# Ten of fourteen own products a layer as three products of 12-bit parts, in a three-layer graph network

## The chip, the core and the metric

The kernel runs on one core of one Trainium2 chip. The metric is the device time of the whole kernel in microseconds (us), the median of several runs. Its engines work side by side, each through its own list of instructions in a fixed order: TensorE (PE in the profile) multiplies matrices, VectorE (DVE) and ScalarE (ACT) work element by element, GpSimd (POOL) and SyncE (SP) here mostly issue transfers (DMA). They wait for each other by semaphores.

## The reference

A layer norm and a relu of x (2500 nodes of 256 numbers), three graph convolutions over the given 80000 edges, and a product of the four stages' results with Wf, added to x. Cut to what matters:

```python
def _edge_conv(x, src, dst, W, b):
    xi, xj = x[dst], x[src]
    m = jnp.concatenate([xi, xj - xi], axis=-1) @ W + b
    s = jax.ops.segment_sum(m, dst, num_segments=N)
    cnt = jax.ops.segment_sum(jnp.ones((dst.shape[0],), m.dtype), dst, num_segments=N)
    return s / jnp.maximum(cnt, 1.0)[:, None]
for W, b in ((W0, b0), (W1, b1), (W2, b2)):
    h = jax.nn.relu(_edge_conv(h, src, dst, W, b))
    xs.append(h)
return x + jnp.concatenate(xs, axis=-1) @ Wf + bf
```

With A the matrix that counts the edges from node to node, a layer is the relu of A times (h Wb) / cnt plus h (Wt - Wb): the second term, a node's product with its own features, is what this text calls an **own product**.

## The kernel before, in words

The nodes are cut into five groups of up to 504; the last ("alone") has 486. Layer 0 builds A from sorted edges with matmuls of one-hot matrices and multiplies at once. It stores A in device memory, the groups 0 to 3 as bf16, the last as f32. Layers 1 and 2 read it back. Every f32 value that multiplies A is held as two f32r parts, `zh` (high) and `zl` (the rest), so that a product with A is two f32r matmuls.

Each of the layers 1 and 2 has two phases.

*The node turns* (`for i in range(Q + LAG)`, 12 turns for 10 pairs of node tiles). A turn multiplies 256 nodes' features by the layer's weights (`Nodes.multiply`, from parts that `split` has made two turns before), takes the results (`parts`, `combine`, `sums`: into zh, zl and their combinations sh, sl) and multiplies the lone group two turns behind (`Alone.multiply`). The lone group's blocks of A are loaded by `load_first` and `load_alone`.

*The stream* (`Stream.run`, 70 steps). The groups 0 to 3 are two pairs. For each pair a Strassen-like scheme uses seven products instead of eight, named by their block of A: b11, b21 and b22 are blocks, r1 to r4 sums and differences of blocks. A pair is 35 steps: five times (c = 0 to 4) the seven products; step n belongs to pair n // 35, c = n // 7 % 5, product n % 7. A step is four matmuls of one 128x504 block, high and low of two node tiles. Results stay in seven PSUM banks over the five c; at c = 4 `take` adds each into hT, the next layer's features, and closes with two Relus.

The order is written out by hand and kept on every engine (all helper operations go through one line, 282, hence L282 in the profile). At step n of `Stream.run`:
- `make(n + LEAD + 1)`, LEAD 5: the block of step n + 5 is made from the staged bf16 blocks: for b11, b21, b22 a cast on ACT, for r1 and r2 an add on DVE and then a cast on ACT, for r3 and r4 one operation on DVE. There are seven block buffers. When a c is used up, a later staged load is issued on SP (`load`).
- at c = 2, `own_sum` makes the sums r1 to r4 of hT that belong to the products' own terms (DVE).
- `multiply`: PE. At c = 4 the own product comes ahead of the four matmuls, as one fp32 matmul (two instructions in the profile) of `ws` or `wsum` with hT or a sum.
- `take` at c = 4.
- `tick(n)`: work that is due at a step: wsum's sums at 3, the features' parts for the next node turns (`split`, one ACT and two DVE operations) at 49, 56, 63 and 65, the parts of the next weights (`Forms`) at 64 to 67, and, in layer 2, the load of the output sums `acc` from device memory at 28 and 42.

After layer 2 a last loop multiplies hT by the last rows of Wf and adds it to `acc` (`add_to_acc`), and the rows go out.

f32r parts of 12 bits: high is the value scaled and rounded to f32r, low the rest, `across` a mix of both; three f32r products of such parts with three of the weight give the fp32 product. Layer 0 already does its own products of the groups 1 to 4 so (`split_own`, `own_forms`, tiles own_h and own_w).

Of the kernel before, what the change touches and what calls it, by code (L numbers as in the profile page):

```python
# [313 lines left out]
def by_windows(ctx: ExitStack, tc: tile.TileContext, x, src, dst, Ws, bs, Wf, bf, out, missing):  # L314
# [3 lines left out]
    P = 128  # L318
# [60 lines left out]
        return ps[-1].tile([P, 512], F32, name="bank")  # L379


    acc = const.tile([P, NT, D], F32, name="acc")
    hT = const.tile([P, DC, NP], F32, name="hT")

    zh = const.tile([P, 2, Q * D + 32], F32R, name="zh")
    zl = const.tile([P, 2, Q * D + 32], F32R, name="zl")
    key_m = early.tile([P, NW + 1, CH, REP], BF16, name="key_m")
    key_n = early.tile([P, NW + 1, CH, REP], BF16, name="key_n")
    away = early.tile([P, WG, CAP], BF16, name="away")
# [5 lines left out]
    ident_b = const.tile([P, P], BF16, name="ident_b")  # L395
    iota_m = const.tile([P, P], BF16, name="iota_m")
    iota_n = const.tile([P, NB], BF16, name="iota_n")
    deg = const.tile([P, WG, W + 1], F32, name="deg")
    gsum = const.tile([P, WG, W + 5], F32, name="gsum")
    nc_ = const.tile([P, W + 2], F32, name="nc_")  # L400
    deg_b = const.tile([P, WG, W + 1], BF16, name="deg_b")
    below = const.tile([P, CH, WG], F32, name="below")
    back_b = const.tile([P, P + 1], BF16, name="back_b")

    const.tile([P, 16], F32, name="between")
    pairs = [(0, 1), (2, 3)]
# [763 lines left out]
    def any_bank():  # L1170
        return next_bank(1, 8)

    tmps = ctx.enter_context(tc.tile_pool(name="tmps", bufs=6))
    stage = ctx.enter_context(tc.tile_pool(name="stage", bufs=4))
    late = ctx.enter_context(tc.tile_pool(name="late", bufs=1))
    sh = late.tile([P, 2, Q * D + 32], F32R, name="sh")
    sl = late.tile([P, 2, Q * D + 32], F32R, name="sl")
    wsum = late.tile([P, 4, P], F32, name="wsum")


    M3, S5, S2, M4 = range(4)
# [4 lines left out]
    def tmp():  # L1186
        return tmps.tile([P, 512], F32, name="tmp")
# [15 lines left out]
    def add_to_acc(t, po):  # L1203
        DVEo.scalar_tensor_tensor(acc[:, t, :], po, share[:, t:t + 1], acc[:, t, :], op0=OP.mult, op1=OP.add)

    class Nodes:

# [34 lines left out]
    def part_of(what, z, j):  # L1242
        if what[0] == "x":
            return tile_of((zh, zl)[z], 2 * j + what[2])[:, what[1] * P:(what[1] + 1) * P]
        return sums_of((sh, sl)[z], j)[:, what[1] * P:(what[1] + 1) * P]

    class Pair:

        def __init__(self, l, i):
            self.l, self.i = l, i  # L1250
            self.one, self.two = (slice(c0, c0 + n) for c0, n in map(group_of, pairs[i]))
            self.bank, self.r = {}, {}
# [38 lines left out]
        def multiply(self, c, part, what, made):  # L1291
            if c == 0:
                self.bank[what] = any_bank()[:, :GS]
            to = self.bank[what]
            if c == Q // 2 - 1:
                if part[0] == "x":
                    w = ws[self.l][0][:, part[2], part[1] * P:(part[1] + 1) * P]
                else:
                    w = wsum[:, part[1], :]
                m = {"b11": hT[:, 0, self.one], "b21": hT[:, 1, self.one], "b22": hT[:, 1, self.two]}.get(what)  # L1300
                PEo.matmul(to, w, self.r[what] if m is None else m, start=False, stop=False)
            for k, j in enumerate((2 * c, 2 * c + 1)):
                for z in range(2):
                    unit[0] = PEo.matmul(to, part_of(part, z, j), made[what][:, k, :],
                                         start=(c == 0 and k == 0 and z == 0),
                                         stop=(c == Q // 2 - 1 and k == 1 and z == 1))

        def take(self, what):
            m, one, two = self.bank.pop(what), self.one, self.two
# [49 lines left out]

    loaded = {}  # L1360

    def load_first(order):
        c = order[0] // 2
        st = stage.tile([P, 4 * GS], F32R, name="staged").rearrange("p (t n) -> p t n", n=GS)
        SPo.dma_start(st.bitcast(F32), a_dram[alone][:, 4 * c:4 * c + 4, :])
        for p in range(2):
            q = order[p] % 2
            loaded[p] = st[:, 2 * q:2 * q + 2, :]

    def load_alone(p, order):  # L1370
        loaded[p] = block()[:, :, :GS]
# [12 lines left out]
    class Stream:  # L1384
# [33 lines left out]
    def split(q):  # L1418
        tile_ = stage.tile([P, 4 * GS], F32R, name="staged")
        Split(q, [tile_[:, k * 2 * D:(k + 1) * 2 * D] for k in range(3)])  # L1420

    begun = []
    for l in range(1, L):
        order = orders[l]
        lone = Alone(l, order)
        if l == 1:
            load_first(order)
            split(order[2])
        pending = []
        stream = Stream(l)  # L1430
        for i in range(Q + LAG):
            if i < Q:
                q = order[i]
                n = Nodes(l, q)
                n.multiply(splits.pop(q), coming[0])
                if i + 2 < Q:
                    load_alone(i + 2, order)
                n.parts()
                n.combine()
                if i + AHEAD_H < Q and order[i + AHEAD_H] not in splits:  # L1440
                    split(order[i + AHEAD_H])
                pending.append(n)
            if i and pending:
                pending.pop(0).sums()
            if 0 < i <= DC:
                lone.own(i - 1, 0)
            if i >= LAG:
                lone.multiply(i - LAG)
            if i == Q - 1:
                stream.load(3)  # L1450
        stream.make(2)
        lone.end()
        turn_of[1] = 0
        if l + 1 < L:
            load_b(l + 1, SPo)
            load_wb(l + 1, SPo)
            load_wt(l + 1, SPo)
        load_wf(l + 1, SPo)
        after = orders[l + 1]

        def tick(n):
            if n == 68 and l + 1 == L:
                begun.append(split_in_blocks(6, False))
            if l == 1 and n % 7 == 6 and n < 28:
                add_bf(n // 7)
            if l + 1 == L and n in (28, 42):
                t = (n - 28) // 14 * Q
                SPo.dma_start(acc[:, t:t + Q, :], acc_dram[:, t:t + Q, :])
            if n == 3:
                combine(wsum, ws[l][0].rearrange("p c (o n) -> p (c o) n", o=2))  # L1470
            if n == 40 and l + 1 < L:
                DVEo.tensor_sub(ws[l + 1][0], ws[l + 1][0], ws[l + 1][1])
            if n in (49, 56):
                split(after[(n - 49) // 7])
            if n == 63 and l + 1 < L:
                load_first(after)
# [12 lines left out]
        stream.run(tick)  # L1489

    order = orders[L]
    for i, q in enumerate(order):
        po = bank()
        po = [po[:, :D], bank()[:, :D] if i == Q - 1 else po[:, D:]]
        for k in range(2):
            if q in PLAIN:
                for c in range(DC):
                    PEo.matmul(po[k], hT[:, c, (2 * q + k) * P:(2 * q + k + 1) * P], wfs[L][:, c, :],
                               start=(c == 0), stop=(c == DC - 1))
            else:  # L1500
                times(po[k], splits[q], k, coming[0])
        for k in range(2):
            t = 2 * q + k
            add_to_acc(t, po[k])
            n = P if t < NT - 1 else LAST
            if i < Q - 4 and q < Q - 1:
                if k:
                    d = SPo.dma_start(out[(t - 1) * P:(t + 1) * P, :].rearrange("(k p) d -> p k d", p=P),
                                      acc[:, t - 1:t + 1, :])
            else:  # L1510
                d = (ACTo if i >= Q - 4 and k else SPo).dma_start(out[t * P:t * P + n, :], acc[:n, t, :])
            if i == Q - 2:
                near_end = d
        if i == 0:
# [52 lines left out]
```

## Time and profile before

| what | us |
|---|---|
| median of 3 runs (lowest, highest) | 462.22 (461.98, 462.48) |
| the profiled execution | 462.09 |
| its span, first to last instruction | 460.2 |
| PE busy | 452.0 (98%) |
| DVE busy | 353.2 (77%) |
| ACT busy | 308.9 (67%) |
| stream of layer 1, from its first step to the next layer's first product | 238.9 to 315.3 |
| stream of layer 2 | 363.7 to about 440 |

How to read it: "busy" is the union of an engine's instructions. Matmuls overlap in the pipeline and their ends are modelled, so what a matmul costs is read from the distance of two starts. A row of the groups gives out<-in by the program's names, shape and count, then busy us and the mean ns of one, then the idle time of the engine ahead of them and what ended it. A row of the timeline gives start, length (of a merged run of equal instructions), and in brackets the idle time ahead of it. The chain that ended last is followed back from the end. The granted TensorE clock is 1.00 throughout.

### The profile page before, as it was taken

What the parts mean: (1) busy time and instruction counts of PE and PEld (TensorE: products, weight loads), DVE (VectorE), ACT (ScalarE), POOL (GpSimd) and SP (SyncE); (2) the same over time, 40 slices, a digit from 0 to 9 for tenths busy, and PEclk for the clock granted to TensorE, in tenths of its full rate; (3) what the DMA queues carried; (4) which work ended last, traced back from release to release, by engine and by line L of the source; (5) the groups of instructions that cost most, each with busy time, mean ns of one, the idle gap of its engine ahead of it and who ended that gap; (6) DMA issues with size and microseconds to landing.
All of it is one profiled execution on the core that took longest, in us unless ns stands there. A gap on an engine that the chain in (4) does not pass through costs nothing.

```text
span 460.2 us, 7512 instructions
## 1 busy us (share of the span) xinstructions
PE 452.0 (98%) x2729; PEld 356.6 (77%) x2729; DVE 353.2 (77%) x676; ACT 308.9 (67%) x595; POOL 62.6 (14%) x95
## 2 busy tenths in 40 slices
PE   8999999999999999999999999999999999999995
PEld 4888877677778778878878868867788787688685
DVE  7999979899888946178758758886877487569795
ACT  4878878694945434377769839756776897597540
POOL 4770006101001000022151000000212000000000
PEclk9999999999999999999999999999999999999999
DMA  8320088982908249685899999626578957520014
GB/s 277 101 58 13 1 171 130 204 174 42 184 1 168 60 171 432 230 231 118 208 333 183 193 186 208 110 90 184 66 154 215 354 184 291 204 92 0 1 64 164
DMA packets 30489, 71.90 MB, mean 156 GB/s; under 512 B 2427, under 2 KB 19150, under 8 KB 29550
## 3 DMA queue, kind: packets, MB, share of 16 engines
q1 hardware_dynamic: 17886, 47.71, 31.3%
q0 software_dynamic: 10784, 21.77, 28.7%
q10 hardware_dynamic: 1776, 1.89, 1.2%
q8 instruction: 22, 0.36, 0.3%
q14 instruction: 21, 0.17, 0.1%
HBM read 45.45 MB, written 28.69 MB: 161 GB/s over the span
## 4 chain that ended last, share of the span: by engine, by line
PE 94%; DVE 2%; DMA 2%; issue 0%; SPq 0%; DVEq 0%
PE bank L282 86%; PE pz L282 8%; DMA wbf<-in_L_gnn_Wf_dram 2%; PE turned L282 1%; DVE one_n L282 1%; DVE one_m L282 1%; DVE own_h L282 0%; DVE hT L282 0%; SPq L282 0%; DVE deg L282 0%; DVE acc L282 0%; DVE away L282 0%; DVE deg_b L282 0%; DVEq L282 0%
## 5 line engine op out<-in xcount | busy, mean ns | idle before, releaser
L282 ACT CAST block<-staged 128x1008 fp32r<-128x1008 bf16 x100 | 97.2, 1031 | 17.0 <-DVE staged L282 6.0
L282 PE MATMUL bank<-a,zh 128*128 128x504 f32 (+1 forms) x200 | 82.0, 410 | 0.0
L282 PE MATMUL bank<-a,zl 128*128 128x504 f32 (+1 forms) x200 | 77.9, 389 | 0.0
L282 PE MATMUL bank<-block,zh 128*128 128x504 f32 (+1 forms) x184 | 76.9, 418 | 0.0
L282 ACT CAST a<-bank 128x480 fp32r<-128x480 f32 (+1 forms) x105 | 54.3, 561 | 31.2 <-PE bank L282 30.9
L282 DVE TENSOR_TENSOR one_m<-iota_m,key_m 128x2048 bf16<-128x2048 bf16 (+2 forms) x55 | 64.1, 1165 | 9.4 <-PE bank L282 9.1
L282 PE MATMUL bank<-block,zl 128*128 128x504 f32 (+1 forms) x184 | 71.2, 387 | 0.0
L282 PE MATMUL bank<-block,sh 128*128 128x504 f32 x160 | 68.9, 431 | 0.0
L282 PE MATMUL bank<-block,staged 128*128 128x512 f32 (+1 forms) x288 | 62.8, 369 | 0.0
L282 PE MATMUL bank<-block,sl 128*128 128x504 f32 x160 | 62.6, 391 | 0.0
L282 PEld LDWEIGHTS bank<-block,staged 128*128 128x128 f32 x288 | 49.3, 188 | 10.2 <-issue 0.9
L282 DVE TENSOR_TENSOR block<-staged 128x1008 fp32r<-128x1008 bf16 x40 | 47.0, 1205 | 5.0 <-PE bank L282 3.5
L282 ACT ACTIVATE tmp<-bank,share 128x256 f32<-128x256 f32 x78 | 34.4, 471 | 23.8 <-PE bank L282 15.9
L282 POOL DMA_DIRECT2D acc_dram<-tmp x20 | 17.1, 853 | 191.9 <-ACT tmp L282 191.9
L282 PEld LDWEIGHTS bank<-a,zh 128*128 128x128 f32 x200 | 37.7, 188 | 6.6 <-ACT a L282 0.3
L282 PEld LDWEIGHTS bank<-a,zl 128*128 128x128 f32 x200 | 37.7, 189 | 6.2 <-issue 0.2
L282 DVE TENSOR_TENSOR one_n<-iota_n,key_n 128x640 bf16<-128x640 bf16 (+2 forms) x110 | 42.5, 428 | 0.0
L282 PEld LDWEIGHTS bank<-block,zh 128*128 128x128 f32 x184 | 34.6, 188 | 9.9 <-issue 2.3
L282 PEld LDWEIGHTS bank<-block,zl 128*128 128x128 f32 x184 | 34.6, 188 | 9.8 <-issue 3.2
L282 DVE TENSOR_TENSOR staged<-staged 128x1008 bf16<-128x1008 bf16 x40 | 27.2, 679 | 18.0 <-ACT block L282 15.8
L282 PEld LDWEIGHTS <-one_m 128*128 128x128 bf16 x834 | 30.3, 98 | 13.7 <-issue 7.0
L282 PE MATMUL pz<-wbf,hT 128*128 128x256 f32 x160 | 38.5, 385 | 0.2 <-DMA wbf<-in_L_gnn_Wf_dram 0.2
(195 smaller groups left out, 676.1 us busy)
## 6 DMA issues: line engine op xcount, KB each, us to landing
staged<-a_dram SPq DMA_DIRECT2D x40, 504.0 KB
a_dram<-a POOLq DMA_DIRECT2D x16, 630.0 KB, 7.8
block<-a_dram SPq DMA_DIRECT2D x16, 504.0 KB
acc_dram<-tmp POOLq DMA_DIRECT2D x20, 256.0 KB, 4.9
a_dram<-a SPq DMA_DIRECT2D x4, 1260.0 KB
acc_dram<-acc SPq DMA_DIRECT2D x1, 2560.0 KB
acc_dram<-in_L_gnn_bf_dram POOLq DMA_DIRECT2D x4, 640.0 KB, 33.2
acc<-acc_dram SPq DMA_DIRECT2D x2, 1280.0 KB
```

Source lines behind the costliest of these rows:

```text
L282: return self.tc.keep_in_program_order(call(*args, **kwargs))
```

## The change

In layers 1 and 2 ten of the fourteen own products are made as three f32r matmuls of parts: all seven of the first pair, and b11, b21 and b22 of the second. The four others stay fp32 at c = 4.
- The weight parts are made by `pair_forms`: for the x products (`ws`) in the node turns 4 and 5, for wsum in the stream at ticks 5 and 7; each is three ACT and two DVE operations of 512 columns.
- The parts of the features are made by `split_own`: one ACT and two DVE operations each. b11 and b21 of the first pair in the node turns 6 and 8; in the stream at the steps of OWN_SPLIT, behind `make`. The first pair's own sums move from c = 2 to these steps.
- The own products come at the c of OWN_AT: the first pair's b11 and b21 at c = 0, b22 and r1 at c = 2, r2 to r4 at c = 4; the second pair's b11, b21, b22 at c = 2.
- The room comes from `acc` (20 KB a partition), which is now held only in layer 0, and from one of four staging buffers. The parts lie in `spare` (three places) and `pair_w`. The output sums are loaded at step 63 of layer 2 into zh and zl, and the last sum goes to a temporary.
- Around it: `load_alone` comes at a turn's end; the first two blocks of layer 2 are loaded as blocks; the splits for the next turns come at 53 and 57 and, in layer 2, 61 and 65.

```diff
-    acc = const.tile([P, NT, D], F32, name="acc")
+    acc = early.tile([P, NT, D], F32, name="acc")
...
-    stage = ctx.enter_context(tc.tile_pool(name="stage", bufs=4))
+    stage = ctx.enter_context(tc.tile_pool(name="stage", bufs=3))
+    spare = late.tile([P, 9 * 512], F32R, name="spare")
+    pair_w = late.tile([P, 3, 2, 4 * P], F32R, name="pair_w")
+    places = [[spare[:, (3 * i + k) * 512:(3 * i + k + 1) * 512] for k in range(3)] for i in range(3)]
...
+    def pair_forms(i, raw):
+        rest = tmp()
+        high, across, last = (pair_w[:, k, i, :] for k in range(3))
+        ACTo.activation(high, raw, AF.Copy, scale=C1 * DOWN)
+        DVEo.scalar_tensor_tensor(rest, raw, C1, high.bitcast(F32), op0=OP.mult, op1=OP.subtract)
+        yield
+        ACTo.activation(across, rest, AF.Copy, scale=E12)
+        DVEo.scalar_tensor_tensor(rest, high.bitcast(F32), -1.0 / E12, rest, op0=OP.mult, op1=OP.add)
+        ACTo.activation(last, rest, AF.Copy, scale=1.0 / C1)
+        yield
+
+    OWN_AT = [{"b11": 0, "b21": 0, "b22": 2, "r1": 2}, {"b11": 2, "b21": 2, "b22": 2}]
+    OWN_SPLIT = [{3: ("b22", 2), 10: ("r1", 0), 14: ("r2", 1), 19: ("r3", 2), 23: ("r4", 0)},
+                 {2: ("b11", 1), 6: ("b21", 2), 10: ("b22", 0)}]
...
+        def split_own(self, what, place):
+            h = self.own_of(what)
+            if h is None:
+                self.own_sum(("r1", "r2", "r3", "r4").index(what))
+                h = self.r[what]
+            high, low, across = self.own[what] = [p[:, :GS] for p in places[place]]
+            ACTo.activation(high, h, AF.Copy, scale=DOWN)
+            DVEo.tensor_sub(low, h, high.bitcast(F32))
+            DVEo.scalar_tensor_tensor(across, low.bitcast(F32), -E12, high.bitcast(F32), op0=OP.mult, op1=OP.add)
...
+            own_at = OWN_AT[self.i].get(what, last)
+            if c == own_at:
+                if what in self.own:
+                    w = (1, part[1]) if part[0] == "s" else (0, 2 * part[2] + part[1])
+                    for k, p in enumerate(self.own.pop(what)):
+                        PEo.matmul(to, pair_w[:, k, w[0], w[1] * P:(w[1] + 1) * P], p, start=(c == 0 and k == 0), stop=False)
...
                 self.make(n + LEAD + 1)
-                if c == 2:
+                if n % 35 in OWN_SPLIT[p.i]:
+                    p.split_own(*OWN_SPLIT[p.i][n % 35])
+                if p.i and c == 2:
                     p.own_sum([w for _, w in SEVEN].index(what) - 2)
...
+            if i + 2 < Q:
+                load_alone(i + 2, order)
+            if i == 4:
+                forms = pair_forms(0, ws[l][0].rearrange("p c n -> p (c n)"))
+                next(forms)
+            elif i == 5:
+                next(forms)
+            elif i in (6, 8):
+                stream.steps[0][1].split_own(("b11", "b21")[i // 2 - 3], i // 2 - 3)
...
-            if l + 1 == L and n in (28, 42):
-                t = (n - 28) // 14 * Q
-                SPo.dma_start(acc[:, t:t + Q, :], acc_dram[:, t:t + Q, :])
+            if l + 1 == L and n == 63:
+                for z, a, b in ((zl, 16, NT), (zh, 0, 8), (zh, 8, 16)):
+                    q = a % 16 // 2
+                    for i in range(2):
+                        SPo.dma_start(z[:, i, q * D:(q + (b - a) // 2) * D].bitcast(F32).rearrange("p (q d) -> p q d", d=D),
+                                      acc_dram[:, a + i:b:2, :])
...
+            if n == 5:
+                sums.append(pair_forms(1, wsum.rearrange("p s n -> p (s n)")))
+                next(sums[0])
+            if n == 7:
+                next(sums.pop())
...
-            if n in (49, 56):
-                split(after[(n - 49) // 7])
-            if n in ((65,) if l + 1 < L else (63, 65)):
-                split(after[2 + (65 - n) // 2])
+            if n in (53, 57):
+                split(after[(n - 53) // 4], 1 + (n - 53) // 4)
+            if n in (61, 65) and l + 1 == L:
+                split(after[2 + (n - 61) // 4], 0 if n == 61 else None)
...
+        sums = tmp().rearrange("p (k d) -> p k d", k=2)
-            add_to_acc(t, po[k])
+            DVEo.scalar_tensor_tensor(sums[:, k, :], po[k], share[:, t:t + 1], acc_of(t), op0=OP.mult, op1=OP.add)
```

More of the change, by code (lines that the diff above doesn't have):

```diff
@@ L1171, in any_bank @@
         return next_bank(1, 8)
+    ctx.enter_context(tc.tile_pool(name="gap", bufs=1)).tile([P, 40], F32, name="between")
     tmps = ctx.enter_context(tc.tile_pool(name="tmps", bufs=6))
-    stage = ctx.enter_context(tc.tile_pool(name="stage", bufs=4))
+    stage = ctx.enter_context(tc.tile_pool(name="stage", bufs=3))
     late = ctx.enter_context(tc.tile_pool(name="late", bufs=1))
+    late.tile([P, 32], F32, name="between")
+    spare = late.tile([P, 9 * 512], F32R, name="spare")
     sh = late.tile([P, 2, Q * D + 32], F32R, name="sh")
     sl = late.tile([P, 2, Q * D + 32], F32R, name="sl")
+    pair_w = late.tile([P, 3, 2, 4 * P], F32R, name="pair_w")
     wsum = late.tile([P, 4, P], F32, name="wsum")
+    places = [[spare[:, (3 * i + k) * 512:(3 * i + k + 1) * 512] for k in range(3)] for i in range(3)]
     M3, S5, S2, M4 = range(4)
@@ L1251, in __init__, with own_of @@
             self.one, self.two = (slice(c0, c0 + n) for c0, n in map(group_of, pairs[i]))
-            self.bank, self.r = {}, {}
+            self.bank, self.r, self.own = {}, {}, {}
+        def own_of(self, what):
+            return {"b11": hT[:, 0, self.one], "b21": hT[:, 1, self.one], "b22": hT[:, 1, self.two]}.get(what)
+        def split_own(self, what, place):
[7 more added lines that the diff above has]
+            DVEo.scalar_tensor_tensor(across, low.bitcast(F32), -E12, high.bitcast(F32), op0=OP.mult, op1=OP.add)
         def load(self, c):
@@ L1294, in multiply @@
             to = self.bank[what]
-            if c == Q // 2 - 1:
-                if part[0] == "x":
-                    w = ws[self.l][0][:, part[2], part[1] * P:(part[1] + 1) * P]
-                else:
-                    w = wsum[:, part[1], :]
-                m = {"b11": hT[:, 0, self.one], "b21": hT[:, 1, self.one], "b22": hT[:, 1, self.two]}.get(what)
-                PEo.matmul(to, w, self.r[what] if m is None else m, start=False, stop=False)
+            last = Q // 2 - 1
+            own_at = OWN_AT[self.i].get(what, last)
[4 more added lines that the diff above has]
+                        PEo.matmul(to, pair_w[:, k, w[0], w[1] * P:(w[1] + 1) * P], p, start=(c == 0 and k == 0), stop=False)
+                else:
+                    if part[0] == "x":
+                        w = ws[self.l][0][:, part[2], part[1] * P:(part[1] + 1) * P]
+                    else:
+                        w = wsum[:, part[1], :]
+                    m = self.own_of(what)
+                    PEo.matmul(to, w, self.r[what] if m is None else m, start=False, stop=False)
             for k, j in enumerate((2 * c, 2 * c + 1)):
@@ L1304, in multiply @@
                     unit[0] = PEo.matmul(to, part_of(part, z, j), made[what][:, k, :],
-                                         start=(c == 0 and k == 0 and z == 0),
-                                         stop=(c == Q // 2 - 1 and k == 1 and z == 1))
+                                         start=(c == 0 and k == 0 and z == 0 and own_at > 0),
+                                         stop=(c == last and k == 1 and z == 1))
         def take(self, what):
@@ L1360, in by_windows, with load_first @@
     loaded = {}
[L1362 to L1365, printed above, removed]
+    def load_first():
+        st = spare[:, :4 * GS].rearrange("p (t n) -> p t n", n=GS)
+        SPo.dma_start(st.bitcast(F32), a_dram[alone][:, 0:4, :])
         for p in range(2):
-            q = order[p] % 2
-            loaded[p] = st[:, 2 * q:2 * q + 2, :]
+            loaded[p] = st[:, 2 * p:2 * p + 2, :]
     def load_alone(p, order):
@@ L1417, in by_windows, with split, acc_of @@
     orders = [None, list(range(Q)), [8, 9, 0, 1, 2, 3, 7, 6, 5, 4], [8, 9, 0, 1, 2, 3, 7, 6, 5, 4]]
[L1418 to L1422, printed above, removed]
+    def split(q, place=None):
+        tile_ = stage.tile([P, 4 * GS], F32R, name="staged") if place is None else None
+        Split(q, places[place] if tile_ is None else [tile_[:, k * 2 * D:(k + 1) * 2 * D] for k in range(3)])
+    def acc_of(t):
+        return tile_of(zh if t < 4 * (Q // 2 - 1) else zl, t % (4 * (Q // 2 - 1))).bitcast(F32)
+    begun, sums = [], []
     for l in range(1, L):
@@ L1426, in by_windows @@
         if l == 1:
-            load_first(order)
+            load_first()
             split(order[2])
@@ L1433, in by_windows @@
                 q = order[i]
+                if i == 0 and l > 1:
+                    load_alone(0, order)
+                    load_alone(1, order)
                 n = Nodes(l, q)
                 n.multiply(splits.pop(q), coming[0])
-                if i + 2 < Q:
-                    load_alone(i + 2, order)
                 n.parts()
@@ L1507, in by_windows @@
                 if k:
-                    d = SPo.dma_start(out[(t - 1) * P:(t + 1) * P, :].rearrange("(k p) d -> p k d", p=P),
-                                      acc[:, t - 1:t + 1, :])
+                    d = SPo.dma_start(out[(t - 1) * P:(t + 1) * P, :].rearrange("(k p) d -> p k d", p=P), sums)
             else:
-                d = (ACTo if i >= Q - 4 and k else SPo).dma_start(out[t * P:t * P + n, :], acc[:n, t, :])
+                d = (ACTo if i >= Q - 4 and k else SPo).dma_start(out[t * P:t * P + n, :], sums[:n, k, :])
             if i == Q - 2:
```

18 lines of the change are left out of this document (7 added, 11 removed).

## The prediction

> **What bounds the kernel now.** I read the chain that ended last first, then the busy time by stage for the two main streams of layers 1 and 2 (70 steps each, two pairs of 35), then the groups by shape and the timeline around single steps. The chain, in order of time (start, length, what):
>
> ```profile
> 128.78 326.36 PE bank L282 x1630
> 455.17 0.48 DVE acc L282
> ```
>
> The four halves of the streams (the first two are layer 1's):
>
> ```profile
> core 0: us, PE busy (x) PEld busy (x) DVE busy (x) ACT busy (x) POOL busy (x), PEclk, DMA share, GB/s
> 239.00:277.00 38.00, 38.00 (x155) 28.56 (x154) 25.99 (x34) 28.00 (x31) 3.00 (x3) 1.00 1.02 192
> 277.00:315.00 38.00, 38.00 (x156) 29.03 (x155) 31.73 (x43) 28.08 (x34) 0.00 (x0) 1.00 0.65 144
> 364.00:402.00 38.00, 38.00 (x155) 28.61 (x154) 26.01 (x35) 27.75 (x31) 0.00 (x0) 1.00 0.69 242
> 402.00:440.00 38.00, 38.00 (x156) 29.03 (x155) 30.91 (x43) 27.38 (x34) 0.00 (x0) 1.00 0.09 28
> ```
>
> From 128.8 to 455.1 the chain is PE alone: whatever PE is spared there is gained, if nothing else becomes late. DVE and ACT are 68 to 84% and 72 to 74% busy in the streams. These are means; what matters is how far ahead of PE each block is ready.
>
> **The own products.** The timeline of PE in plain steps (10 to 12), and at the end of the first pair, where every step holds one fp32 own product:
>
> ```profile
> 247.63 0.39 PE L282 MATMUL bank<-block,sh 128*128 128x504 f32 x1
> ...
> 248.54 0.39 PE L282 MATMUL bank<-block,sh 128*128 128x504 f32 x1
> ...
> 249.45 0.39 PE L282 MATMUL bank<-block,sh 128*128 128x504 f32 x1
> ...
> 266.75 1.01 PE L282 MATMUL bank<-hT,wt 128*128 128x504 f32 x2
> ...
> 268.52 1.00 PE L282 MATMUL bank<-hT,wsum 128*128 128x504 f32 x2
> ```
>
> A plain step takes 248.54 - 247.63 = 0.91 (four matmuls, 0.228 from start to start); one with an own product 1.77. The fp32 product is 0.85. Three matmuls of parts, which in layer 0 take as long as a block's,
>
> ```profile
> L282 PE MATMUL bank<-own_h,own_w 128*128 128x504 f32 (+1 forms) x48 | 13.6, 399 | 0.0
> ```
>
> are 3 x 0.228 = 0.685. Ten a layer in two layers: 20 x 0.17 = **3.4 us less** on PE, which is the whole gain. If PE stays the bound, 462.1 becomes 458.7.
>
> **What the parts cost.** Each of the eight products split inside a stream adds one ACT activation (high) and two DVE operations (low, which needs high, and across, which needs low); the wsum parts (ticks 5 and 7) add three ACT and two DVE operations. Groups of the kinds that they add to, and of those they meet:
>
> ```profile
> L282 ACT CAST block<-staged 128x1008 fp32r<-128x1008 bf16 x100 | 97.2, 1031 | 17.0 <-DVE staged L282 6.0 <-PE bank L282 5.7 <-issue 2.2
> L282 DVE TENSOR_TENSOR staged<-hT,staged 128x512 fp32r<-128x512 f32 x24 | 16.5, 686 | 12.4 <-ACT staged L282 12.4
> L282 DVE SCALAR_TENSOR_TENSOR staged<-staged 128x512 fp32r<-128x512 f32 x24 | 16.6, 692 | 0.8
> L282 ACT ACTIVATE staged<-hT 128x512 fp32r<-128x512 f32 x24 | 15.0, 628 | 2.1 <-DVE block L282 2.1
> L282 DVE TENSOR_TENSOR own_h<-hT,own_h 128x486 fp32r<-128x486 f32 x2 | 1.3, 667 | 4.9 <-ACT own_h L282 4.9
> L282 DVE TENSOR_TENSOR tmp<-tmp,hT 128x504 f32<-128x504 f32 x8 | 5.4, 680 | 0.1
> ```
>
> The second row and the fifth already show the danger: low makes DVE wait for ACT (12.4 us over 24 splits, 4.9 over two own splits of layer 0). DVE is in order, so the blocks r3 and r4 and the adds for r1 and r2 stand behind that wait, and the casts of r1 and r2 on ACT behind the adds. What a split does to its neighbours when two of them meet the own sums shows in the second pair (timeline of DVE, ACT and PE):
>
> ```profile
> 297.01 1.21 DVE L282 TENSOR_TENSOR block<-staged 128x1008 fp32r<-128x1008 bf16 x1
> 298.59 0.69 DVE L282 TENSOR_TENSOR staged<-hT,staged 128x512 fp32r<-128x512 f32 x1 [0.37 <-ACT staged L282]
> 299.32 0.69 DVE L282 SCALAR_TENSOR_TENSOR staged<-staged 128x512 fp32r<-128x512 f32 x1
> 299.93 1.20 DVE L282 TENSOR_TENSOR block<-staged 128x1008 fp32r<-128x1008 bf16 x1
> ```
>
> ```profile
> 297.93 0.62 ACT L282 ACTIVATE staged<-hT 128x512 fp32r<-128x512 f32 x1
> 298.46 2.89 ACT L282 CAST block<-staged 128x1008 fp32r<-128x1008 bf16 x3
> ```
>
> ```profile
> 302.02 0.39 PE L282 MATMUL bank<-block,zh 128*128 128x504 f32 x1
> ```
>
> Block r4 is done at 301.13 and used at 302.02: a lead of 0.9 us, after four own sums (0.68 each) and two splits in 14 steps. The change puts four splits, three own sums and the wsum parts into steps 3 to 19 of a stream, where the lead starts lower still (ACT, DVE and PE from step 2 on):
>
> ```profile
> 239.53 0.58 ACT L282 ACTIVATE hT<-bank 128x486 f32<-128x486 f32 x1 [0.24 <-PE bank L282]
> 240.00 5.69 ACT L282 CAST block<-staged 128x1008 fp32r<-128x1008 bf16 x6
> 245.85 4.78 ACT L282 CAST block<-staged 128x1008 fp32r<-128x1008 bf16 x5 [0.16 <-DVE staged L282]
> ```
>
> ```profile
> 241.06 0.69 DVE L282 TENSOR_TENSOR staged<-staged 128x1008 bf16<-128x1008 bf16 x1 [3.23 <-ACT block L282]
> 241.83 2.33 DVE L282 TENSOR_TENSOR block<-staged 128x1008 fp32r<-128x1008 bf16 x2
> 244.08 0.42 DVE L282 TENSOR_TENSOR wsum<-wt 128x256 f32<-128x256 f32 x1
> 244.53 0.62 DVE L282 TENSOR_TENSOR wsum<-wsum,wt 128x128 f32<-128x128 f32 x2
> 245.07 1.46 DVE L282 TENSOR_TENSOR staged<-staged 128x1008 bf16<-128x1008 bf16 x2
> ```
>
> ```profile
> 241.16 0.42 PE L282 MATMUL bank<-block,sh 128*128 128x504 f32 x1
> ```
>
> Step 2's cast ends at 240.00 + 1.03 = 241.03 and PE takes it at 241.16: lead nothing. The change helps here: the own products of b11 and b21 now precede steps 0 and 1, so PE comes 2 x 0.685 = 1.37 later.
>
> From start to start, by these rows: a cast 0.93 ((5.69 - 1.03) / 5), an r3 or r4 block 1.12 (2.33 - 1.21), low to across 0.73, across to the next 0.61, high to the next cast 0.53, an add 0.6 like across (0.69 long). Hand-overs: ACT to DVE 0.03 (241.03 to 241.06), DVE to a cast 0.1 (245.07 + 0.69 to 245.85), ready block to PE 0.13. A block of seven steps thus needs 4.7 of ACT, 3.45 of DVE and 6.4 of PE; a split adds 0.53 and 1.34, an own sum 0.6 to 0.7 of DVE.
>
> **The ledger, layer 1, first pair.** At step n the code first makes the block of step n+5, then splits; each engine keeps this order.
> - Step 3: ACT's casts run on 0.93 apart from 240.00, so the high of b22 comes at 244.68 to 245.31. DVE is free at 244.16 (241.83 + 2.33) and waits; low 245.34, across 246.06, wsum's sums 246.66 to 247.64 (0.99 as now), the add for r1 until 248.32. Its cast, 248.42 to 249.45, keeps ACT from wsum's high until 249.36 to 249.99. DVE waits again, rest 250.02 to 250.70, the add for r2 until 251.30, its cast until 252.43. PE wants that block (step 11) at 249.45 + 1.37, less 0.07 for today's two short waits ahead of it, 250.75, and gets it at 252.56: **1.8 us lost**. Wsum's across holds DVE once more, and r4 (step 13) costs 0.5.
> - Steps 10 and 14: r1's own sum ends at 255.41, its high comes behind a cast at 256.11, across ends 258.18; adds and r3 until 260.50, r2's own sum until 261.21, high until 261.88, across until 263.31, r4 until 264.43. PE wants it (step 20) at 262.80 and gets it at 264.56: **1.8 us**.
> - Carried on in this way: 0.9 at step 25 (r3's split), 0.3 in crumbs up to step 31. The last block of the pair runs even, and its takes and the two closing Relus leave little lead to the second pair, whose three splits stand in its first 11 steps: 0.3 at steps 39 and 45, and at steps 46 to 48 2.7 (DVE waits from 290.75 to 292.45 for the high of b21, behind the cast of r2). Sum 8.2, less 1.7 saved: **+6.5** in layer 1. Layer 2 has splits at 61 and 65 beside the next forms: the same, less 0.3 at step 46 and 0.6 more at the stream's end, **+6.8**.
>
> The ledger has two sides. Were DVE never to wait for an ACT high, the added work alone would fit: 2.9 us faster. With hand-overs of 0.08 instead of 0.03 it is 14.9 slower; with all durations 3% shorter, 9.7 slower. I take the rows as they stand: 13.3 slower.
>
> A rule to weigh: the rows 299.32 and 299.93 have DVE starting 0.08 before the operation ahead of it ends. [...] The rows decide for 13.3.
>
> **What else moves, at nothing.** The b11 and b21 splits and the first weight parts go into the node turns ahead of the streams, 4.1 us of DVE over five turns:
>
> ```profile
> DVE zl L282 <- ACT zh L282: 22.1, 18, 3.3
> ```
>
> DVE idles 1.2 us a turn there and its results are used two turns later; uncovered it would cost up to 4.1 a layer. Three staging buffers instead of four: a load is issued when the block three before it is consumed, 14 steps (13 us) ahead of need. In layer 1's first pair DMA is saturated (share 1.02), but the queue stays full, so loads land no later; if not, they would hide behind the same stalls. Moving the two block loads of a node turn behind that turn's products leaves them four turns. The output sums come at step 63 instead of 28 and 42:
>
> ```profile
> acc<-acc_dram SPq DMA_DIRECT2D x2, 1280.0 KB
> ```
>
> 2.62 MB at 242 GB/s (the row 364 to 402) is 11 us, with the queue empty (share 0.09) and some 10 us of steps before the first 0.5 MB is read, which go first; SP has nothing behind them but the outputs. Uncovered, 1 us or so. Final sums into a temporary instead of in place: the same DVE operation.
>
> **The sum.** The profiled execution took 462.09 us, 460.2 of span and 1.9 around it, against a median of 462.22. 460.2 - 3.4 + 16.7 = 473.5 of span, **475.4 us**.
>
> **Rivals.**
> - *The parts fit into idle time* (faster): DVE's added 8.2 us (five splits 6.8, wsum's parts 1.4) on 26 of 38 in the first pair do fit on average, at 93%; it decides from the point where each high is done before DVE reaches its low. Then 2.9 to 3.4 faster, 459. Against it: the 12.4 us row. 0.12. Half of it, cancelling the gain: 0.05 for no change.
> - *Only wsum's parts collide little* (the lead at the stream's start grows more than the 1.37 I reckon): with wsum's parts no burden the ledger gives +5.4, 467.5. 0.17.
> - *PE's clock falls*: the granted clock is 1.00 in all four rows, with no PE gap there. Were stalls of 2 us to halve it for some four steps after, a step would take 1.8 instead of 0.9; three such stalls a layer add 3.6 each, 21.6 in all, of which I take half to fall into the ledger's own waits: 486. [...] 0.03.
> - *The ledger*: 0.63.
>
> **How the numbers follow.** The likeliest case gives 475.4, its own bounds 471.8 (3% shorter) to 477 (slower hand-overs). The range goes down to 467, so that it takes in the smaller collision, and up to 481, by the 4.1 of an uncovered node phase; outside are 459, no change and the clock, 0.2. About 0.2% (0.9 us) is what a measurement can tell. Slower 0.63 + 0.17 + 0.03 = 0.83, faster 0.12, same 0.05.
>
> **What would show it.** Own products as three matmuls 0.23 apart (else the 3.4 is wrong); PE with idle time in both streams, ended by ACT and DVE blocks, 8 us a layer, first at step 11 of the stream; DVE waiting for the highs; DVE over 85% busy in both streams. A stream no longer than 75 us, or PE still unbroken, would prove me wrong; so would waits of PE on loads, on the output sums' DMA or in the node turns.

## The result and the profile after

The changed kernel takes **486.29 us** (median of 4 runs, 485.74 to 487.17), the kernel before 462.19 beside it: ratio 1.0523, 95% interval 1.0502 to 1.0543. It is slower by 24.1 us. The forecast was slower by 13.3, and 486 lies outside its range. Of all executions behind this text one stands apart, in experiment 11: 640.88 us at a granted clock of 0.66; without it that median of 462.81 would be 462.76.

The profiled execution of the changed kernel took 485.75 with a span of 483.9. First the shares of the chain that ended last, then the costliest group of ACT and the own products in parts:

```profile
PE 53%; DVE 15%; DMA 11%; issue 10%; ACT 8%; POOL 2%; SPq 0%; ACTq 0%; DVEq 0%; POOLq 0%
```

```profile
L282 ACT CAST block<-staged 128x1008 fp32r<-128x1008 bf16 x100 | 99.1, 1031 | 35.2 <-DVE staged L282 28.2
```

```profile
L282 PE MATMUL bank<-spare,pair_w 128*128 128x504 f32 x60 | 18.4, 415 | 0.0
```

The chain, which was PE alone from 128.8 us on, is now handed from engine to engine. The casts of r1 and r2 wait 28.2 us for DVE's adds, where it was 6.0. The own products are sixty matmuls, as meant. The busy time by phase: node turns of layer 1, its stream from the first own product on, the same for layer 2, and the last loop:

```profile
core 0: us, PE busy (x) PEld busy (x) DVE busy (x) ACT busy (x) POOL busy (x), PEclk, DMA share, GB/s
190.80:240.60 49.80, 49.13 (x210) 38.77 (x208) 37.50 (x74) 36.06 (x76) 10.32 (x13) 1.00 0.82 219
240.60:325.50 84.90, 77.18 (x320) 58.91 (x319) 67.93 (x92) 62.15 (x76) 4.14 (x3) 1.00 0.71 138
325.50:376.20 50.70, 49.65 (x209) 38.62 (x208) 37.80 (x75) 36.74 (x76) 8.56 (x10) 1.00 0.78 196
376.20:462.10 85.90, 80.10 (x322) 61.71 (x320) 66.49 (x93) 61.67 (x77) 0.00 (x0) 0.96 0.36 118
462.10:483.90 21.80, 15.16 (x110) 14.40 (x110) 15.99 (x33) 4.58 (x7) 0.00 (x0) 0.97 0.36 120
```

PE stands still for 7.7 us of the first stream and 5.8 of the second, where the granted clock is 0.96 besides. The same phases before:

| phase | before | after | difference | forecast |
|---|---|---|---|---|
| node turns, layer 1 | 48.35 | 49.80 | +1.45 | 0 |
| stream, layer 1 | 76.34 | 84.95 | +8.6 | +6.5 |
| node turns, layer 2 | 48.45 | 50.7 | +2.25 | 0 |
| stream, layer 2 | 76.6 | 85.9 | +9.3 | +6.8 |
| last loop and end | 19.9 | 21.8 | +1.9 | 0 |

With 0.2 ahead of them that is the 23.7 by which the span grew: 13.3 forecast, 10.4 not. The stream of layer 2 is taken up to the third matmul of the last loop (440.32 and 462.11), ahead of which PE waits 0.37 us in the changed kernel; up to the first (440.09 and 461.34) the last two differences would be +8.8 and +2.5. Step 11, the first stall, in the timelines of PE, DVE and ACT (the brackets give the idle time ahead and what ended it):

```profile
254.44 0.50 PE L282 MATMUL bank<-block,sh 128*128 128x504 f32 x1 [1.81 <-ACT block L282]
```

```profile
249.57 0.68 DVE L282 TENSOR_TENSOR staged<-staged 128x1008 bf16<-128x1008 bf16 x1
251.96 0.69 DVE L282 SCALAR_TENSOR_TENSOR tmp<-wsum,pair_w 128x512 f32<-128x512 f32 x1 [1.71 <-ACT pair_w L282]
252.57 0.68 DVE L282 TENSOR_TENSOR staged<-staged 128x1008 bf16<-128x1008 bf16 x1
```

```profile
250.36 1.04 ACT L282 CAST block<-staged 128x1008 fp32r<-128x1008 bf16 x1 [2.20 <-DVE staged L282]
251.30 0.63 ACT L282 ACTIVATE pair_w<-wsum 128x512 fp32r<-128x512 f32 x1
253.36 1.03 ACT L282 CAST block<-staged 128x1008 fp32r<-128x1008 bf16 x1 [1.43 <-DVE staged L282]
```

Read it in order of time: DVE's add for r1 (249.57), its cast (250.36), behind that on ACT wsum's high (251.30), for which DVE waits 1.71 us (251.96), behind that on DVE the add for r2 (252.57), its cast (253.36), and PE at 254.44. This is the forecast chain link by link, 1.9 us later than forecast, 1.6 of it because the stream began later. PE waits 1.81 us, the figure forecast.

### The profile page after: what moved, and what is told of

It reads as the page before. It is cut to its first block, busy times and chain, and to the rows that moved or that the text cites. A ratio compares the mean times of both kernels' runs of the same rounds, so it can differ in the third digit from the quotient of the medians.

```text
span 483.9 us, 7649 instructions
## 1 busy us (share of the span) xinstructions
PE 458.2 (95%) x2749; PEld 360.9 (75%) x2749; DVE 383.1 (79%) x724; ACT 324.4 (67%) x627; POOL 62.8 (13%) x95
## 4 chain that ended last, share of the span: by engine, by line
PE 53%; DVE 15%; DMA 11%; issue 10%; ACT 8%; POOL 2%; SPq 0%; ACTq 0%; DVEq 0%; POOLq 0%
PE bank L282 44%; PE pz L282 7%; ACT block L282 4%; DMA acc_dram<-acc 4%; DMA acc_dram<-tmp 3%; DVE tmp L282 3%; DVE staged L282 3%; DMA staged<-a_dram 3%; DVE spare L282 2%; DVE block L282 2%; POOL acc_dram L282 1%; ACT tmp L282 1%; ACT spare L282 1%; PE turned L282 1%; DMA acc<-in_x_dram 1%
## 5 line engine op out<-in xcount | busy, mean ns | idle before, releaser
L282 ACT CAST block<-staged 128x1008 fp32r<-128x1008 bf16 x100 | 99.1, 1031 | 35.2 <-DVE staged L282 28.2
L282 PE MATMUL bank<-block,sh 128*128 128x504 f32 x160 | 67.3, 421 | 10.3 <-ACT block L282 6.5
L282 PE MATMUL bank<-block,zl 128*128 128x504 f32 (+1 forms) x192 | 75.1, 391 | 0.5 <-DVE zl L282 0.5
L282 PE MATMUL bank<-block,staged 128*128 128x512 f32 (+1 forms) x228 | 53.7, 383 | 0.2 <-DVE staged L282 0.2
L282 PEld LDWEIGHTS bank<-block,sh 128*128 128x128 f32 x160 | 30.5, 190 | 23.5 <-ACT block L282 12.3
L282 PEld LDWEIGHTS bank<-block,staged 128*128 128x128 f32 x228 | 40.2, 188 | 10.4 <-DVE staged L282 2.0
L282 PEld LDWEIGHTS bank<-block,zh 128*128 128x128 f32 x192 | 36.5, 190 | 14.5 <-DVE block L282 4.8
L282 PEld LDWEIGHTS bank<-block,zl 128*128 128x128 f32 x192 | 36.6, 191 | 8.9 <-DVE zl L282 1.1
```

Source lines behind the costliest of these rows:

```text
L282: return self.tc.keep_in_program_order(call(*args, **kwargs))
```

## The experiments

All edits are to the changed kernel unless another is named. Times are medians; each ratio is to the kernel before, run beside it.

**1. No parts at all (e1).** `OWN_AT` and `OWN_SPLIT` empty, own sums at c = 2 for both pairs, no `pair_forms`; the rest of the change stays.

> All own products are fp32 at c = 4 again and no parts are made, of weights or of features; all the rest of the change stays (three staging buffers, the late load of the output sums, the temporary for the final sums, the block loads at a turn's end, the feature splits of the next turns at 53, 57, 61 and 65). Theory A (the parts cost it all: DVE's lows wait for ACT's highs): 462.2 +- 0.7, streams of 76.4 and 76.6 us, the end as before. Rival B (the room costs a part of it): the 1.9 us that the end has lost, the 0.9 at step 39 or the 1.5 and 2.3 of the node turns stay, 464 to 468.

467.25 us, ratio 1.0103 (1.0088 to 1.0119). Theory A alone falls: without one part made, 5 us stay. The trace is of the slowest of the six executions, 470.01. In it the end and layer 1's node turns are as before (19.9 and 48.35), layer 2's node turns are 0.5 longer, and the loss lies in layer 1's stream, 84.0 instead of 76.3. First SP's staged loads from the fourth on, in the kernel before and in this one; then ACT and PE at step 21; then the DMA queues from 246 to 254 us, in this kernel and in the kernel before:

```profile
234.81 47.67 SPq L282 DMA_DIRECT2D staged<-a_dram  x14
```

```profile
244.09 31.44 SPq L282 DMA_DIRECT2D staged<-a_dram  x10
```

```profile
262.06 2.90 ACT L282 CAST block<-staged 128x1008 fp32r<-128x1008 bf16 x3 [9.72 <-DMA staged<-a_dram]
```

```profile
263.15 0.79 PE L282 MATMUL bank<-block,zh 128*128 128x504 f32 x1 [4.54 <-ACT block L282]
```

```profile
q0 software_dynamic: 501, 0.50, 96.9%
q1 hardware_dynamic: 24, 0.02, 1.1%
```

```profile
q1 hardware_dynamic: 349, 1.23, 55.0%
q0 software_dynamic: 347, 0.34, 42.7%
```

The fourth load goes to SP's queue (q1) at 244.09 us, when its buffer is free, instead of 234.81. But for 8 us the DMA engines do little else than GpSimd's queue (q0). That is the bias rows: four transfers of 640 KB (`add_bf`) that add them to the output sums in device memory. The program has them at steps 6, 13, 20 and 27 of layer 1's stream, but nothing holds them there, and GpSimd issues them from 235.35 to 242.23. ACT's cast waits 9.72 us for the load, PE 4.54, and the granted clock is 0.50 from 262.46 to 269.28.

**2. Low and across two steps later (e2).** What stands ahead of the `yield` runs at the step of the split, what follows it two steps later:

```diff
             ACTo.activation(high, h, AF.Copy, scale=DOWN)
+            yield
             DVEo.tensor_sub(low, h, high.bitcast(F32))
```

> Every split inside a stream is cut in two: own sum and ACT's high at the step of the change, DVE's low and across two steps later; the same instructions, the same places, the same c of the products. Theory A (what costs is that the low waits for the high at the head of DVE's queue): by the ledger the streams lose 0.7 us instead of 8.2 and 1.0 instead of 8.5, so 7.1 less in each, 486.3 - 14.2 = 472.1, and DVE waits for the highs no more. Rival C (the added work itself is too much for DVE and ACT): the work is the same, so 485 or more.

470.27, ratio 1.0184 (1.0165 to 1.0204): 16.0 us less from an edit that changes nothing but the order on DVE. The work rival falls. DVE's waits for the highs in the second stream, changed kernel first, became fewer, though they aren't gone as expected:

```profile
DVE spare L282 <- ACT spare L282: 11.7, 9, 2.1
```

```profile
DVE spare L282 <- ACT spare L282: 4.2, 4, 1.7
```

That stream is now 76.15 us long, shorter than before, and the mean granted clock of the traced execution is 0.998, where the changed kernel's is 0.991, so the 16.0 us include the price of the clock (experiment 4); the first, with the late load of experiment 1, is 79.35.

**3. The third weight part a turn later (e3).**

```diff
-        rest = tmp()
+        rest = tmp() if i else wsum.rearrange("p s n -> p (s n)")
...
         DVEo.scalar_tensor_tensor(rest, high.bitcast(F32), -1.0 / E12, rest, op0=OP.mult, op1=OP.add)
+        if i == 0:
+            yield
         ACTo.activation(last, rest, AF.Copy, scale=1.0 / C1)
...
-            elif i == 5:
+            elif i in (5, 6):
                 next(forms)
-            elif i in (6, 8):
+            if i in (6, 8):
```

> In the node turns the third weight part of the x products (ACT, from DVE's second result) comes at turn 6 instead of at the end of turn 5, and its temporary is wsum's place, not one of the six. Theory D (the node turns are late because ACT waits 2.5 us there for DVE, and everything on ACT behind it, zf and the final sums with their DMA, comes late): the turns get back to 48.4 us, 1.45 + 2.26 = 3.7 less, of which I expect 3: 483.3. Rival E (the splits of b11 and b21 at turns 6 and 8 or the loads make them late): no change, 486 +- 0.5.

481.55, ratio 1.0413 (1.0394 to 1.0432). The wait in the changed kernel (ACT), the two waits of PE at the end of the turns, and the two node turns with the edit (the columns as above):

```profile
220.45 0.63 ACT L282 ACTIVATE pair_w<-tmp 128x512 fp32r<-128x512 f32 x1 [2.46 <-DVE tmp L282]
...
235.67 0.47 ACT L282 ACTIVATE tmp<-bank,share 128x256 f32<-128x256 f32 x1 [4.54 <-DMA acc_dram<-tmp]
```

```profile
236.94 0.49 PE L282 MATMUL bank<-block,zh 128*128 128x486 f32 x1 [0.44 <-ACT zh L282]
237.66 0.49 PE L282 MATMUL bank<-block,zl 128*128 128x486 f32 x1 [0.24 <-DVE zl L282]
```

```profile
190.60:238.90 48.30, 48.30 (x209) 38.89 (x208) 37.49 (x74) 37.03 (x77) 11.30 (x13) 1.00 0.82 223
326.00:374.90 48.90, 48.72 (x209) 38.81 (x208) 37.80 (x75) 37.64 (x77) 8.56 (x10) 1.00 0.77 199
```

The second row shows how far the 2.46 us reach: the final sums behind them come late, so does their accumulating DMA, and the last turn's zf waits 4.54 us for the buffer that it frees (2.50 before the change, 2.06 with the edit). With the edit the turns take 48.3 and 48.9 us. That is 1.5 and 1.8 less, 3.3 together. The trace is of the slowest of the five executions, 483.45, and only 2.3 below the traced one of the changed kernel: its first stream takes 87.1 instead of 84.9. So 3.3 is measured in the turns, and why the medians differ by 4.7 I can't place.

**4. PE fed in two stalls (e4).** Ahead of the blocks of steps 11 and 47:

```diff
+    FILL = (0, 1, "r2"), (1, 1, "r3")
...
+            if (self.i, c, what) in FILL:
+                idle = any_bank()[:, :GS]
+                for k in range(8):
+                    PEo.matmul(idle, zh[:, 0, :P], zh[:, 0, :GS], start=(k == 0), stop=(k == 7))
```

> Eight matmuls of zh with itself into an unused bank (1.8 us, their result is read by nobody) stand ahead of the block products of steps 11 and 47 in both streams, where PE stands still for 2.06 and 2.17 us. Theory F (the pauses halve the clock in the second stream, 3.41 us each time, and this is why it is longer than the first and than the ledger): granted clock 1.00 in all stages, 1 to 1.7 us less, 484.9. Rival G (the steps after a pause wait for ACT and DVE anyway): no change, 486.3 +- 0.4. Slower than that only if a pause was shorter than 1.8 us.

484.27, ratio 1.0471 (1.0451 to 1.0491): 2.0 us less by 32 matmuls more. Stretches of 3.41 us of the changed kernel's second stream, and the whole second stream of this one (the columns as above):

```profile
386.93:390.34 3.41, 1.60 (x7) 0.92 (x6) 2.49 (x3) 1.98 (x4) 0.00 (x0) 1.00 0.00 0
390.34:393.75 3.41, 3.41 (x9) 2.68 (x9) 2.40 (x3) 2.65 (x5) 0.00 (x0) 0.50 0.14 17
393.75:397.16 3.41, 3.41 (x16) 2.78 (x16) 2.64 (x4) 2.20 (x4) 0.00 (x0) 1.00 0.77 286
431.30:434.71 3.41, 1.71 (x7) 1.18 (x8) 3.38 (x5) 2.40 (x4) 0.00 (x0) 1.00 0.00 0
434.71:438.12 3.41, 3.41 (x10) 2.69 (x9) 3.20 (x5) 1.97 (x2) 0.00 (x0) 0.50 0.87 281
```

```profile
376.70:461.00 84.30, 81.03 (x338) 62.12 (x336) 66.44 (x93) 61.47 (x77) 0.00 (x0) 1.00 0.37 121
```

The two stretches in which PE stands still for 1.81 and 1.70 us are each followed by one at clock 0.50, with 9 and 10 matmuls in it, where the stretch from 393.75 at 1.00 has 16. Fed, PE keeps 1.00, and the stream is 84.3 instead of 85.9. Theory F holds.

**5. No parts, bias rows late (e5).** `add_bf` at steps 28, 35, 42 and 49, each made to wait for the step's last matmul.

> The kernel without parts (all own products fp32 at c = 4, the rest of the change kept), which took 467.25 us, with one more edit: the four transfers that add the bias rows to the output sums in device memory wait for steps 28, 35, 42 and 49 of layer 1's stream instead of starting ahead of it. Theory S (with three staging buffers the fourth load of a stream is issued only at 244 us instead of 235, and then stands behind the bias rows' transfers, which are in the DMA engines alone from 248 to 254; PE waits 4.5 us for it at step 21 and its clock halves): the load lands in time, 462.2 +- 0.6. Rival H (three buffers are one too few in any case): PE still waits at step 21 or later, 465 or more.

470.3, ratio 1.0162 (1.0147 to 1.0178): a miss, and what rival H expected; experiments 9 and 11 decide against H. PE no longer waits at step 21, but 1.5 and 2.8 us at steps 56 and 59, for casts that wait for loads again, 7.3 us at the longest, and the mean granted clock of the traced execution is 0.992. Moved, the bias rows meet other loads, as long as each of the four transfers is 640 KB.

**6. Experiment 2, and the next features earlier (e6).** In layer 2 the splits for the last loop at 50, 57, 58 and 64.

> The kernel with low and across two steps later (470.27 us), and in layer 2 the four feature splits for the last loop at steps 50, 57, 58 and 64 instead of 53, 57, 61 and 65. Theory I (the last loop is DVE's: own products that left c = 4 took 2.6 us of PE time out of the last seven steps, DVE ends them 2.3 us after PE instead of 0.65 and never catches up): by the ledger 2.2 us less, 468.1. Rival J (the last loop is longer for another reason, the temporary or the late output sums): no change, 470.3 +- 0.5.

468.9, ratio 1.0159 (1.0141 to 1.0177); 1.4 below experiment 2. The executions of the two overlap (468.68 to 471.16 and 469.67 to 472.34), so the traces are the better measure: the last loop takes 20.25 us instead of 21.8 (expected: 2.2 less in all). DVE's last addition into hT of the stream (before, then changed) shows what it mends. The last loop's third matmul, from which its length is counted here, is at 440.32 and 462.11:

```profile
440.29 0.68 DVE L282 TENSOR_TENSOR hT<-bank,tmp 128x504 f32<-128x504 f32 x1
```

```profile
464.35 0.68 DVE L282 TENSOR_TENSOR hT<-bank,tmp 128x504 f32<-128x504 f32 x1
464.94 0.86 DVE L282 SCALAR_TENSOR_TENSOR tmp<-bank,share,zl 128x256 f32<-128x256 f32 x2
```

Against that matmul, DVE ends the stream 2.3 us later than before and never catches up, since the last loop keeps it busy (16.0 of 21.8). Three own products had left the last seven steps, and with them 2.6 us of PE time beside which DVE had finished.

**7 and 8. All parts placed anew, with the bias rows late (e7) or as in the change (e8).** The ledger, turned round, looks for steps at which no block is late even if all operations take 6% longer: the splits' pieces apart and two to six steps behind each other, b22 and r1 used at c = 3, the weight parts one operation at a time. With experiment 3's edit.

```diff
+    OWN_AT = [{"b11": 0, "b21": 0, "b22": 3, "r1": 3}, {"b11": 2, "b21": 2, "b22": 3}]
+    SUM_AT = {2: (0,), 8: (1,), 12: (2, 3), 39: (0, 1), 40: (3,), 61: (2,)}
+    HIGH_AT = {15: (("b22", 1),), 16: (("r1", 0), ("r2", 2)), 24: (("r4", 1),), 25: (("r3", 0),),
+               41: (("b11", 1),), 44: (("b21", 0),), 51: (("b22", 0),)}
+    LOW_AT = {17: ("b22",), 18: ("r1",), 22: ("r2",), 26: ("r4",), 30: ("r3",), 43: ("b11",), 47: ("b21",), 54: ("b22",)}
+    FORMS_AT = (5, 9, 11, 13, 14)
+    NEXT_HIGH, NEXT_LOW, NEXT_IN = (47, 60, 55, 60), (51, 62, 58, 62), (2, 0, 1, None)
...
```

> All twenty products in parts, every step of their making placed anew by the ledger so that no block is late even with durations 6% longer: own sums at 2 to 12, highs at 15 to 25, lows two to six steps behind them, weight parts from 5 to 14 one operation at a time, pair 2 likewise, b22 and r1 used at c = 3; the third weight part of the node turns a turn later; the bias rows late. Theory A with its additions (waits at the head of in-order queues, the load, the node turns and the end, and nothing else): streams of 74.9 us from the first own product instead of 76.4, node turns and end as before, 462.1 - 3.4 = 458.7. Rival C (the work itself is too much): 462 or more, with DVE and ACT busy where PE waits.

463.83, ratio 1.0032 (1.0022 to 1.0043). The second stream takes the 74.9 expected; the first 77.3, late at steps 56 to 58 for loads, and the second node turns 50.5 instead of 48.45, where PE waits 1.2 us in all for the feature splits. These are some 4.4 of the 4.6 us by which the traced execution (463.28) missed what was expected. Experiment 9, which moves only the bias rows, has neither.

> The planned kernel with the bias rows where the change has them, ahead of layer 1's stream. Theory S: the fourth load lands at 262 to 264 as in the kernel without parts, PE wants it at step 21 near 260, so 4 us are lost there and the clock halves behind it: 463 to 466. Rival H': the load is no later than before, 458.7 +- 0.5.

464.96, ratio 1.0055 (1.0043 to 1.0067), inside what theory S expected: PE waits 2.6 us at step 21, and the mean granted clock of the traced execution is 0.989, where experiment 7's is 0.999.

**9. The same plan, bias rows in twenty transfers (e9).** 128 KB each, one behind every sixth step of both streams.

```diff
-            if l == 1 and n % 7 == 6 and n < 28:
-                add_bf(n // 7)
+            if n % 6 == 3 and n < (66 if l == 1 else 54):
+                d = add_bf(n // 6 + (0 if l == 1 else 11))
+                tc.add_manual_dep(d.ins, unit[0].ins.name, ...)
```

> The planned kernel with the bias rows' four transfers of five tiles cut into twenty of one tile (128 KB each), one behind every sixth step of both streams (eleven in layer 1, nine in layer 2). Theory S (staged loads come late wherever 10 us of bias rows stand in the DMA engines with only three buffers): no staged load is late any more, streams of 74.9 us each from the first own product, second node turns 48.9, 459.1 in all. Rival H'' (three buffers are too few for layer 1's traffic however it is spread): still 2 us or more lost to loads, 461 or more.

**459.48 us**, ratio 0.9941 (0.9928 to 0.9955): faster than both kernels.

```profile
190.70:239.00 48.30, 48.30 (x208) 38.92 (x207) 37.49 (x74) 37.02 (x77) 8.49 (x10) 1.00 0.82 223
239.00:313.70 74.70, 74.70 (x320) 59.99 (x319) 66.89 (x92) 61.42 (x75) 9.01 (x11) 1.00 0.56 143
313.70:362.60 48.90, 48.72 (x209) 38.83 (x208) 37.81 (x75) 37.40 (x76) 8.59 (x10) 1.00 0.79 200
362.60:437.50 74.90, 74.90 (x322) 60.17 (x321) 67.84 (x96) 61.57 (x78) 7.33 (x9) 1.00 0.55 153
437.50:457.60 20.10, 14.87 (x112) 14.25 (x110) 13.94 (x29) 3.94 (x6) 0.00 (x0) 0.93 0.40 130
```

PE is busy in every microsecond of both streams, while DVE is busy for 66.9 of 74.7 and 67.8 of 74.9, as long as in the changed kernel (67.9 and 66.5). The work was never too much; it stood in the wrong order.

**10. No parts, four staging buffers (e10).** `bufs=4` and no `pair_w`.

> The kernel without parts (467.25 us) with four staging buffers again (the room of the weight parts, which aren't made there, gives the place); bias rows as in the change. Theory S': the third buffer too few is all that the room costs, so 462.2 +- 0.4. Rival B (the moved block loads, the late output sums or the temporary cost as well): 463 or more.

462.71, ratio 1.0008 (0.9999 to 1.0017): 4.5 less than with three, 0.1 above the band expected, and theory S' holds. The 0.5 left over lies in the second node turns (48.9 against 48.45), as in experiment 1; they were 48.9 with experiment 3's edit too.

**11. No parts, three buffers, bias rows in twenty (e11).**

> The kernel without parts, three staging buffers, with the twenty small transfers of the bias rows. Theory S: 462.4 +- 0.6, so that the planned kernel beside it shows what the parts themselves bring, 3.4 less. Rival H'': loads still late, 464 or more.

462.81, ratio 1.0012 (1.0003 to 1.0021). The loads are late no more, with three buffers: rival H'' falls. Beside experiment 9 the parts bring 462.81 - 459.48 = 3.3 us.

**12. The four single edits together (e12).** Experiments 2, 3 and 6 and the twenty transfers.

> The changed kernel with the four single edits together and nothing else replaced: low and across two steps later, the third weight part of the node turns a turn later, layer 2's splits for the last loop at 50, 57, 58 and 64, the bias rows in twenty transfers. If the causes are these four and add up: 470.3 (low later) less 3.3 (node turns) less 1.9 (end) less 2.5 (the load in layer 1's first pair), 462.6. If they hide behind each other, 464 or more.

461.62, ratio 0.9984 (0.9975 to 0.9993), 1.0 less than expected: the causes do not hide behind each other, and together they hold all of the 24.1 us; and the changed kernel's own plan, so mended, is a little faster than before. Experiment 9 has the rest, the short stalls that are left here at steps 31, 39 and 46.

## Why the prediction was wrong, and where it was right

- **The saving of 3.4 us on PE: right.** A step with an own product in parts takes 1.60 us (0.91 + 0.69), and experiments 9 and 11 differ by 3.3.
- **The ledger's mechanism: right.** Step 11 shows it, and experiment 2 takes it away. The signs named for it came: PE's idle time of 7.7 and 5.8 us, first at step 11, and DVE waiting for the highs. The stalls of layer 1, read from the distance of two steps, against those forecast: step 11 2.1 (1.8), 13 0.45 (0.5), 20 1.9 (1.8), 25 1.5 (0.9), 39 0.9 (0.3, with step 45), 46 to 48 2.6 (2.7). DVE operations start 0.08 us before the one ahead ends here too (251.96 + 0.69 against 252.57).
- **"PE's clock falls", chance 0.03: the step that was weighed wrongly.** The time came out at that rival's 486, but not by its price, so this is chance: it costs 2.0 us, not 10.8. I called every stall too short for it, which no trace showed: in the kernel before, PE stands still nowhere in the streams. Here waits of 1.81 and 1.90 us, at steps 11 and 47 of the second stream, were each followed by 3.41 us at 0.50.
- **"What else moves, at nothing": the step that failed.** *Node turns*: I counted DVE's added time and its idle time, not that ACT would wait at the head of its own queue for DVE: 3.3 us by experiment 3. Waits of PE in the node turns stood among the signs of being wrong, and they came. *The end*: I looked at the final sums' operations, not at when DVE comes to them. PE's time saved in the last seven steps is given back as DVE's lag, 1.9 us, of which experiment 6 took back 1.6. *Three staging buffers*: "the queue stays full, so loads land no later" is refuted by experiments 1 and 10: by itself the missing buffer costs 467.25 - 462.71 = 4.5 us, and nothing once the bias rows go in small transfers (experiment 11, 462.81). That "they would hide behind the same stalls" held for most of it. ACT's waits for loads in the changed kernel's first stream (total, times, longest):

```profile
ACT block L282 <- DMA staged<-a_dram: 1.8, 2, 1.1
```

  These 1.8 us are near the 2.1 that this stream lost beyond the ledger. The longer wait is ahead of the casts of 267.03; behind them on ACT is r3's high (268.90), for which DVE waits 1.25 us, then DVE's add (270.94), its cast (271.73) and step 25 (272.81), whose stall was 0.6 longer than forecast. So this wait does stand in the chain of a stall; what a load in time would save in the changed kernel was not tried alone.
- **The range** took the 4.1 of an uncovered node phase as one upper bound for all terms set to nothing. They came together: 3.7 in the node turns, 1.9 at the end, and 4.6 in the streams, of which the clock is some 2, and the late loads may be most of the rest.
- **The sign for "DVE over 85% busy" was wrong:** 80% and 77%. A stall makes a stream longer as well, so a waiting engine looks less busy. Experiment 9 has 90%, and no stall.

## What to carry to other kernels

Work that fits an engine's idle time on average can still cost several times what it saves (16.0 us by experiment 2, for 3.3 saved), if one of its operations waits at the head of an in-order queue for another engine: issue the operation that is waited for some steps ahead, and place the pieces by a ledger that carries both queues. An item "at nothing" needs the same check in both directions, who waits for whom in which queue, for transfers too; and time saved on the bound engine in a program's last steps is lost if another engine needed that time to finish (1.9 us here).

## What the runs showed of the hardware

- **Two pauses of PE were followed by half its clock, two others as long were not.** In the changed kernel's second stream PE waits 1.81 us ahead of 390.10 (step 11) and 1.90 ahead of 433.00 (step 47). The granted clock is 0.50 from 390.34 to 393.75 and from 434.71 to 438.12, 3.41 us each time, and 1.00 in the 3.41 behind them. In its first stream PE waits 1.81 us ahead of 254.44 and 1.90 ahead of 298.71, at the same two steps, and 1.73 ahead of 266.69, and the clock is 1.00 throughout (row 240.60). In experiment 1 PE waits 4.54 us ahead of 263.15, and the clock is 0.50 for 6.82 us from 262.46. Why the same pauses halved the clock in one stream and not in the other, these runs don't show.
- **A load issued beside another queue's backlog came late.** In experiment 1 SP issued the load at 244.09 us. From 246 to 254 us its queue moved 24 of 525 packets, 1.1% of the DMA engines' time, and GpSimd's queue took 96.9%; the cast that waited for the load began at 262.06. In the kernel before, 246 to 254 us held 349 packets of SP's queue and 347 of GpSimd's (55.0% and 42.7%). Why SP's queue got so little in experiment 1 was not shown.
